# Hybrid attention and experts on one core: token scales carried through DRAM, and third layers that catch up every other step

## The chip, the cores and the metric

The kernel runs on one core of a Trainium2 chip. The metric is the device time of one execution in microseconds. The kernel before takes 3328.4 us (median of three runs, 3327.84 to 3328.48). Its profile shows an execution of 3332.1 us.

The core has five engines that run side by side, each in its own program order: TensorE (PE in the profile, with its weight loads as PEld), VectorE (DVE), ScalarE (ACT), GpSimd (POOL) and SyncE (SP), which here only issues transfers. Data is float32 throughout.

## The reference, cut to what matters

The input is eight images of 256 channels by 32 x 32 pixels. Layer 0 is a pooled attention. Layer 1 turns each image into 1024 tokens of 256 channels, and adds an attention and then a mixture of eight experts:

```
t = tokens(x)                                   # (8, 1024, 256)
t = t + attn(ln_t(t))                           # one head of 256
t = t + ffn(ln_t(t))
ln_t(v): (v - mean) / sqrt(var + 1e-5)          # over the 256 channels of a token
attn(h): softmax(q k^T / 16) v,  q, k, v = h W^T + b
ffn(h):  w = softmax(mean_b(h) Wr + br)         # (1024, 8), one gate per token and expert
         y_e = relu(bn(relu(bn(h W1_e)) W2_e)) Wo_e + bo_e
         sum over e of w_e y_e
```

The change touches the division by the standard deviation in both ln_t, and the order in which the experts' third layer (Wo_e) is worked off.

## The kernel before

A tile of t holds channels in the partitions (two blocks of 128) and tokens along the free dimension. So a token's factor 1/sqrt(var + eps) has to be multiplied into every partition of one column. The mean needs no work here, since it is folded into the weights that follow.

scale_tokens does this. TensorE transposes the tile, VectorE takes statistics of each token (bn_stats), and statistics ends with the power -0.5 on GpSimd. The result r has tokens in the partitions: r[p, t] belongs to token 128 t + p. To turn it into a row that all partitions have, GpSimd builds diag, the identity times r, and TensorE multiplies it by a matrix of ones. Every output row then holds the factors of 128 tokens for each block, in PSUM. VectorE multiplies the tile by it. There are two callers. layer1 scales a whole image of 1024 tokens (two products of 512 columns). norm scales a quarter of 256 tokens after attention (one product of 256 columns, four times an image).

The program is written out by a planner. Work comes in generators (threads) that yield what they need next: an engine, the tiles that have to be ready, and for TensorE a PSUM slot. The class Flow keeps an expected time for every engine and tile (note, cost), and its order becomes the order of the instructions; each engine then works strictly in that order. For a transfer, note adds a lag after its issue until its tile counts as ready.

The attention of layer 0 sets the beat. Its loop has 384 steps: eight images, two channel groups, two halves, twelve blocks of keys. In each step TensorE forms four score products (sc), ScalarE takes their exponential (pt), and TensorE multiplies the block before by the values (pv). After each step f.step lets the threads put in other work up to a credit: convolutions and norms of the next image, and layer 1 of the images that are done (keys "y,t", values "p,v", 32 quarters in all). What is not placed by the end of the loop comes in a tail, where the experts already start so that TensorE is filled. The exponentials' sums are formed on VectorE and, for part of the blocks, by accumulating transfers issued on GpSimd's queue (pt<-pt).

The experts run in units of one expert and 512 tokens, 128 units. first7 and second are the first two layers, in seven half-width products (a Strassen form) of 256 columns each; early ones use a plain form of four products of 512. sums puts the seven products together on VectorE, and combined forms the differences for the next layer, on GpSimd or VectorE. third is the third layer. It needs the gates, which need all images' tokens, so at the end of the tail some 25 units have their first two layers done and wait, stored in DRAM (h2d). The main loop of experts then works off this backlog: weighed fetches, multiplies by the gate (weigh) and combines, and thirds runs one third layer. While the backlog is larger than two (many), every second layer is followed by an extra third layer.

Of the kernel before, what the change touches and what calls it, by code (L numbers as in the profile page):

```python
# [11 lines left out]
ALU = mybir.AluOpType  # L12
# [4 lines left out]
P = 128  # L17
C = 256
HW = 1024
# [636 lines left out]
class Flow:  # L656
# [90 lines left out]
    def note(self, engine, op, ins, args, kwargs):  # L747
        aps = [a for a in (*args, *kwargs.values()) if hasattr(a, "tensor") or hasattr(a, "space")]
        out = kwargs.get("out", args[0] if args else aps[0])
        srcs = [a for a in aps if a is not out]  # L750
        prev = self.last.get(engine)
        if prev is not None:
            self.tc.add_manual_dep(
                ins.ins,
                prev,
                mybir.DependencyInfo(mybir.DependencyClass.NoSync, mybir.DependencyReason.DATA),
                reason="program order",
            )
        self.last[engine] = ins.ins.name
        start = self.now[engine]  # L760
        names = [n for a in srcs for n in self.keys(a)]
        outs = self.keys(out)
        for n in (*names, *outs):
            if self.writer.get(n) != engine:
                start = max(start, self.ready.get(n, 0.0))
        for o in outs:
            if self.reader.get(o, engine) != engine:
                start = max(start, self.read.get(o, 0.0))
        cost = self.cost(engine, op, out, srcs)
        if engine == "PE":  # L770

            tiling = None if op == "transpose" else self.tiling(srcs)
            if tiling != self.tiled:
                cost += {None: 0.09, "rows": 0.2, "columns": 0.13}[tiling]
                self.tiled = tiling

        wide = [a for a in srcs if a.space != PSUM and a.free_size() > 4]
        if "dma" not in op and engine == "POOL" or engine == "DVE" and wide and (len(wide) > 1 or op in ("tensor_scalar", "tensor_copy")):
            start = max(start, self.port)
            self.port = start + cost  # L780
        self.now[engine] = end = start + cost
        lag = 0.15
        if "dma" in op:
            size = 4e-3 * out.shape[0] * out.free_size() if out.space != DRAM else 4e-3 * srcs[0].shape[0] * srcs[0].free_size()
            lag = 2.0 + 0.0045 * size if engine == "SP" else 1.5 + 0.0078 * size
        for n in {*outs, self.key(out)}:
            self.ready[n] = max(self.ready.get(n, 0.0), end + lag)
            self.writer[n] = "DMA" if "dma" in op else engine
        self.open.difference_update(names)
        for n in {*names, *map(self.key, srcs)}:  # L790
            self.read[n] = max(self.read.get(n, 0.0), end + lag)
            self.reader[n] = engine
# [85 lines left out]
        return need[0] is not None and (need[2] is None or self.free(need[2]) < NEVER)  # L878


def attention(tc, kit, f, outer, ended, nb, consts, x, t1, t2, hn, bounds, vecs, q_t, kv_t, proj_t, gqk_t, wqk, wqkv, vecs1, w1_d, w1c, gate_d, wrc, vecs2, bnvec):

# [5 lines left out]
    with ExitStack() as ctx:  # L888
        l1, shared = outer
# [4 lines left out]
        def T(pool, shape, tag, bufs=1):  # L894
            return f.tile(pool, shape, tag, bufs=bufs)
# [60 lines left out]
        def mix():  # L956
# [43 lines left out]
            r = T(wp, [P, 2], "war")  # L1000
# [19 lines left out]
            for c in range(2):  # L1020
                f.pe.transpose(ps[:, c * P : (c + 1) * P], bd[:, c, :], ident)
            yield ve(ps)
            bdt = T(l1, [P, 2, P], "diag4")
            f.ve.tensor_copy(bdt, ps[:, :C].rearrange("p (c q) -> p c q", c=2))
            yield pe(bdt, tag="sm")
            ps = small()
# [36 lines left out]

        def pool(*tiles):
            return "POOL", tiles, None

        def until(cond):
            return None, cond, None
# [168 lines left out]
        def statistics(st, n, eps, mean=None):  # L1237


            var = T(l1, [P, n], f"var{n}")  # L1240
            dev = T(l1, [P, n], f"dev{n}")
            if mean is not None:
                f.ve.tensor_tensor(mean, st[:, :, 1], st[:, :, 4], ALU.add)
            f.ve.tensor_tensor(dev, st[:, :, 1], st[:, :, 4], ALU.subtract)
            f.ve.tensor_tensor(var, st[:, :, 2], st[:, :, 5], ALU.add)
            f.ve.tensor_tensor(dev, dev, dev, ALU.mult)
            f.ve.scalar_tensor_tensor(var, dev, C / 4.0, var, ALU.mult, ALU.add)
            r = T(l1, [P, n], f"rstd{n}", bufs=3)
            rstd(r, var, eps, 1.0 / C)
            return r  # L1250
# [292 lines left out]
                f.sp.dma_start(t1[b], last)  # L1543
            projected[0] += 1

        def scale_tokens(src, n):

            tiles = n // P
            st = T(l1, [P, tiles, 6], f"st{tiles}")
            for g in range(0, tiles, 2):  # L1550
                yield pe(src, tag="sm")
                ps = small()
                for u in range(2):
                    for c in range(2):
                        o = u * C + c * P
                        f.pe.transpose(ps[:, o : o + P], src[:, c, (g + u) * P : (g + u + 1) * P], ident)
                yield ve(ps)
                for u in range(2):
                    f.ve.bn_stats(st[:, g + u, :], ps[:, u * C : (u + 1) * C])
            yield ve(st)  # L1560
            r = statistics(st, tiles, 1e-5)
            for g in range(0, tiles, 4):
                m = min(4, tiles - g)
                yield pool(r)
                diag = T(l1, [P, m, P], f"diag{m}")
                f.pool.tensor_tensor(
                    diag,
                    ident[:, None, :].to_broadcast([P, m, P]),
                    r[:, g : g + m].unsqueeze(2).to_broadcast([P, m, P]),
                    ALU.mult,  # L1570
                )
# [11 lines left out]
        def layer1():  # L1583

            for b in range(nb):
                yield until(lambda: projected[0] > b and ready)
                t = T(l1, [P, 2, HW], "t")
                f.sp.dma_start(t, t1[b])
                yield from scale_tokens(t, HW)
                yield until(lambda: written[0] >= 4 * b)  # L1590
                v = T(l1, [P, 8, C], "v")
                for g in range(4):
# [91 lines left out]

        def norm(b, q, o):

            yield from scale_tokens(o, C)
            f.sp.dma_start(hn[b][:, :, q], o)
            scaled[0] += 1
            written[0] += 1  # L1690
            ended[0] = written[0] // 4
# [123 lines left out]
        for i in range(len(steps) + 1):  # L1815
            if i < len(steps):
                b, c, half, kc = steps[i]
# [171 lines left out]
def experts(tc, kit, nb, t2, hn, h2d, w1c, w2_d, wo_d, bnvec, bo_d, gate_d, wrc, consts8, gtd, out, f, outer, ended, early):  # L1989
# [12 lines left out]
    with ExitStack() as ctx:  # L2002
        l1, shared = outer
# [4 lines left out]
        T = f.tile  # L2008
# [330 lines left out]
        while n3 < total:  # L2339
            many = n2 > n3 + 2  # L2340
            if n2 < n1 - 1 or n1 == total and n2 < total:
                second(n2, many)
                n2 += 1
                if many:
                    weighed(f.pool)
                    thirds()
            weighed(f.ve if many else f.pool)
            if n1 < total:
                first7(n1)
                n1 += 1  # L2350
            thirds()
# [3 lines left out]
def tile_conv_attn_hybrid(  # L2355
# [41 lines left out]
    bnvec = T(cpool, [P, 4 * 2 * NE], "bnvec")  # L2397
    bounds = [T(cpool, [P, NBOUND], f"bound{i}") for i in range(2)]
    flag = T(cpool, [P, 1], "flag")
    last = partial(experts, tc, kit, nb, t2, hn, h2d, w1c, w2_d, wo_d, bnvec, bo_d, gate_d, wrc, consts8, gtd, out)  # L2400
    with ExitStack() as early:
        l1 = early.enter_context(tc.tile_pool(name="l1", bufs=1, side="right"))
        shared = early.enter_context(tc.tile_pool(name="psum_l1", bufs=1, space=PSUM, side="right"))
        f = Flow(tc, kit)

        ended = [0]
        attention(
            tc, kit, f, (l1, shared), ended, nb,
            consts, x, t1, t2, hn, bounds, vecs0, q_t, kv_t, proj_t, gqk_t, wqk, wqkv, vecs1, w1_d, w1c, gate_d, wrc, vecs2, bnvec,
        )  # L2410
        last(f, (l1, shared), ended, early)
# [122 lines left out]
```

## Time and profile before

| stage | from, us | to, us | TensorE busy, us | VectorE busy, us |
| --- | --- | --- | --- | --- |
| start | 0 | 400 | 316.0 | 277.0 |
| attention of layer 0 with layer 1 between | 400 | 1975 | 1510.9 | 1207.2 |
| change to the tail | 1975 | 2050 | 62.7 | 33.7 |
| tail of layer 1 with experts | 2050 | 2280 | 230.0 | 112.9 |
| catch-up of third layers | 2300 | 2575 | 262.1 | 249.4 |
| experts in step | 2625 | 2900 | 274.0 | 216.9 |

In the lines below, the part with numbers 1 to 40 slices the span; a digit is the busy share of a slice in tenths. A line of a stretch gives its length, then for each engine the busy time and in brackets the number of instructions, the granted clock of TensorE, the share of the transfer engines and GB/s. A line of a group gives the engine, the operation, output and inputs by name, the shapes, the count, the busy time, the mean of one in ns and the idle time just before. A line of transfers gives the issuing queue, the count, the size and the time from issue to landing. A TensorE product of float32 is recorded as two pieces, and a piece's recorded length overlaps the next one's. All operations carry the line of the planner's helper, L669, so one goes by the names of tiles.

### The profile page before, as it was taken

The numbers are of one execution on the slowest core, as the hardware profiler recorded it, in microseconds if no ns is written. First come the engines' busy times: TensorE is split into PE (matmuls) and PEld (weight loads), VectorE is DVE, ScalarE is ACT, GpSimd is POOL, SyncE is SP. The second block draws the span as 40 slices with busy tenths as digits, with TensorE's granted clock in tenths as the row PEclk, the third lists the DMA queues.
The fourth block names the chain that finished last, engine by engine and source line by source line (L and its number), as shares of the span: only waits on it lengthen the run. The fifth ranks groups of instructions, "written<-read, shape, count | busy, mean of one in ns | idle before, by whom it ended". The sixth has DMA issues, their size and how long they took to land.

```text
span 3332.1 us, 42942 instructions
## 1 busy us (share of the span) xinstructions
PE 3137.4 (94%) x15970; PEld 1912.8 (57%) x15970; DVE 2472.4 (74%) x4069; ACT 1734.4 (52%) x2328; POOL 1227.3 (37%) x1300
## 2 busy tenths in 40 slices
PE   8687899999999999899899999999999999999997
PEld 4332244344344344344345346777888888888886
DVE  5687788786887886886884555446998787787776
ACT  4476676666576566576566543333233444444442
POOL 2211413213213214213211112006666776777775
PEclk9798999999999999999999999999999999999999
DMA  2357656656646646656556656124442010000000
GB/s 74 82 121 158 131 106 146 133 101 154 133 100 157 135 104 147 135 120 123 121 125 133 133 119 237 70 88 159 158 146 102 20 45 26 20 20 32 20 13 21
DMA packets 106666, 347.10 MB, mean 104 GB/s; under 512 B 13056, under 2 KB 38408, under 8 KB 83216
## 3 DMA queue, kind: packets, MB, share of 16 engines
q0 software_dynamic: 28608, 179.85, 28.1%
q1 hardware_dynamic: 74480, 162.45, 14.1%
q8 instruction: 128, 2.10, 0.3%
q10 hardware_dynamic: 3360, 1.97, 0.2%
q14 instruction: 90, 0.74, 0.1%
HBM read 105.11 MB, written 73.97 MB: 54 GB/s over the span
## 4 chain that ended last, share of the span: by engine, by line
PE 57%; DVE 5%; issue 3%; ACT 3%; POOL 3%; DMA 2%; SPq 0%; DVEq 0%; POOLq 0%; ACTq 0%
PE bank L669 18%; PE sm L669 13%; PE y L669 8%; PE sc L669 6%; PE sx L669 6%; PE pv L669 5%; DVE h L669 2%; ACT pt L669 2%; POOL tm L669 1%; DVE u L669 1%; DMA pt<-pt 1%; ACT h L669 1%; POOL t L669 1%; DVE t L669 1%; DVE c L669 1%
## 5 line engine op out<-in xcount | busy, mean ns | idle before, releaser
L669 ACT ACTIVATE pt<-sc 128x2048 f32<-128x2048 f32 (+1 forms) x384 | 719.9, 1875 | 326.5 <-PE sc L669 272.7
L669 DVE SCALAR_TENSOR_TENSOR acc<-p,vec,acc 128x225 f32<-128x225 f32 (+7 forms) x928 | 526.6, 574 | 29.3 <-ACT acc L669 4.8
L669 PE MATMUL sc<-q,kn 32*128 32x512 f32 (+1 forms) x3072 | 445.6, 650 | 94.7 <-ACT pt L669 92.9
L669 DVE TENSOR_TENSOR pt<-pt,pt 128x1024 f32<-128x1024 f32 x320 | 387.4, 1254 | 144.3 <-DMA pt<-pt 135.3
L669 POOL DMA_DIRECT2D pt<-pt x192 | 174.0, 907 | 780.1 <-ACT pt L669 615.7
L669 PE MATMUL pv<-pt,vt 128*32 128x512 f32 (+1 forms) x3072 | 420.6, 620 | 0.0
L669 ACT ACTIVATE p1c<-bank 128x256 f32<-128x256 f32 x228 | 87.2, 383 | 576.4 <-PE bank L669 576.1
L669 ACT ACTIVATE h<-h,bnvec 128x512 f32<-128x512 f32 x456 | 345.0, 805 | 50.7 <-DVE h L669 43.7
L669 POOL TENSOR_TENSOR rstd<-rstd,mhalf 128x4 f32<-128x4 f32 (+2 forms) x88 | 107.0, 1216 | 673.8 <-DVE rstd L669 635.0
L669 DVE TENSOR_TENSOR h<-p1c,bank 128x512 f32<-128x512 f32 x228 | 155.2, 681 | 194.7 <-PE bank L669 191.2
L669 PEld LDWEIGHTS sc<-q,kn 32*128 32x128 f32 (+1 forms) x3072 | 116.1, 178 | 285.8 <-ACT pt L669 184.9
L669 POOL TENSOR_TENSOR tm<-h,tm 128x256 f32<-128x256 f32 x206 | 247.6, 1202 | 16.1
L669 DVE TENSOR_TENSOR h<-u,bank 128x256 f32<-128x256 f32 x456 | 232.1, 550 | 7.9
L669 PEld LDWEIGHTS pv<-pt,vt 128*32 128x32 f32 (+1 forms) x3072 | 60.7, 108 | 301.7 <-issue 290.3
L669 POOL TENSOR_TENSOR tm<-h 128x512 f32<-128x512 f32 x103 | 133.9, 1300 | 245.2 <-ACT h L669 241.2
L669 DVE TENSOR_TENSOR h<-h,gate 128x1024 f32<-128x1024 f32 x128 | 209.1, 1642 | 2.5 <-DMA h<-h 2.1
L669 PE MATMUL bank<-h,w2e 128*128 128x256 f32 (+1 forms) x612 | 198.8, 453 | 4.1 <-DVE h L669 4.1
L669 PE MATMUL y<-t,s3e 128*128 128x256 f32 x768 | 188.0, 381 | 10.6 <-POOL t L669 10.3
L669 POOL TENSOR_TENSOR t<-h,t 128x256 f32<-128x256 f32 x210 | 177.4, 845 | 16.5
L669 PE MATMUL bank<-t,s1e 128*128 128x256 f32 x750 | 182.3, 379 | 0.0
L669 PE MATMUL sm<-y,t 128*128 128x256 f32 x752 | 180.6, 385 | 0.0
L669 DVE TENSOR_TENSOR u<-h,bank 128x512 f32<-128x512 f32 x228 | 156.7, 687 | 24.0
(316 smaller groups left out, 5604.3 us busy)
## 6 DMA issues: line engine op xcount, KB each, us to landing
pt<-pt POOLq DMA_DIRECT2D x160, 1024.0 KB, 7.4
h<-h SPq DMA_DIRECT2D x90, 512.0 KB, 3.2
xi<-in_x_dram SPq DMA_DIRECT2D x16, 512.0 KB, 6.7
t<-t SPq DMA_DIRECT2D x8, 1024.0 KB, 9.7
res<-t SPq DMA_DIRECT2D x32, 256.0 KB, 3.9
t<-res SPq DMA_DIRECT2D x32, 256.0 KB, 5.4
hn<-res SPq DMA_DIRECT2D x32, 256.0 KB, 3.0
hn<-hn SPq DMA_DIRECT2D x16, 512.0 KB, 4.2
```

Source lines behind the costliest of these rows:

```text
L669: ins = fn(*args, **kwargs)
```

## The change

It has two parts. For the first six images, scale_tokens no longer forms diagonals. SyncE stores r into a row in DRAM in token order, and loads it back broadcast to all 128 partitions (256 or 512 tokens at a time, into one buffer named rb); VectorE multiplies by that. TensorE and GpSimd have no part in it. The last two images keep the diagonal products, which answer sooner. The planner is told to count 8 us for each of these transfers. The diag tiles of the remaining cases move into the same buffer rb.

In the experts, the extra third layer comes only with every other second layer while a backlog is there, and VectorE and GpSimd change places in who combines for it.

```
 def scale_tokens(src, n, b):
     ...
     r = statistics(st, tiles, 1e-5)
+    if b < nb - 2:
+        row = kit.tile(dram, [1, n], f"dev_row{kit.n}")
+        yield sp(r)
+        f.sp.dma_start(row.rearrange("o (t p) -> (o p) t", p=P), r)
+        yield sp(row)
+        w = min(512, n)
+        for o in range(0, n, w):
+            rb = T(l1, [P, w], "rb")
+            f.sp.dma_start(rb, row[:, o : o + w].to_broadcast([P, w]))
+            yield ve(rb)
+            d = src[:, :, o : o + w]
+            f.ve.tensor_tensor(d, d, rb[:, None, :].to_broadcast([P, 2, w]), ALU.mult)
+        return
     for g in range(0, tiles, 4):
         m = min(4, tiles - g)
         yield pool(r)
-        diag = T(l1, [P, m, P], f"diag{m}")
+        diag = T(l1, [P, m, P], "rb")
         ...
 # Flow.note
             lag = 2.0 + 0.0045 * size if engine == "SP" else 1.5 + 0.0078 * size
+            if "dev_row" in (self.key(out) + "".join(map(self.key, srcs))):
+                lag = 8.0
 ...
 # main loop of experts
                 second(n2, many)
                 n2 += 1
-                if many:
-                    weighed(f.pool)
+                if many and n2 % 2:
+                    weighed(f.ve)
                     thirds()
-            weighed(f.ve if many else f.pool)
+            weighed(f.pool)
```

More of the change, by code (lines that the diff above doesn't have):

```diff
@@ L878, in possible, with attention @@
         return need[0] is not None and (need[2] is None or self.free(need[2]) < NEVER)
-def attention(tc, kit, f, outer, ended, nb, consts, x, t1, t2, hn, bounds, vecs, q_t, kv_t, proj_t, gqk_t, wqk, wqkv, vecs1, w1_d, w1c, gate_d, wrc, vecs2, bnvec):
+def attention(tc, kit, f, outer, ended, nb, dram, consts, x, t1, t2, hn, bounds, vecs, q_t, kv_t, proj_t, gqk_t, wqk, wqkv, vecs1, w1_d, w1c, gate_d, wrc, vecs2, bnvec):
     nc = tc.nc
@@ L1022, in mix @@
             yield ve(ps)
-            bdt = T(l1, [P, 2, P], "diag4")
+            bdt = T(l1, [P, 2, P], "rb")
             f.ve.tensor_copy(bdt, ps[:, :C].rearrange("p (c q) -> p c q", c=2))
@@ L1065, in pool, with sp @@
             return "POOL", tiles, None
+        def sp(*tiles):
+            return "SP", tiles, None
         def until(cond):
@@ L1544, in project, with scale_tokens @@
             projected[0] += 1
-        def scale_tokens(src, n):
+        def scale_tokens(src, n, b):
             tiles = n // P
@@ L1588, in layer1 @@
                 f.sp.dma_start(t, t1[b])
-                yield from scale_tokens(t, HW)
+                yield from scale_tokens(t, HW, b)
                 yield until(lambda: written[0] >= 4 * b)
@@ L1685, in norm @@
         def norm(b, q, o):
-            yield from scale_tokens(o, C)
+            yield from scale_tokens(o, C, b)
             f.sp.dma_start(hn[b][:, :, q], o)
@@ L2407, in tile_conv_attn_hybrid @@
         attention(
-            tc, kit, f, (l1, shared), ended, nb,
+            tc, kit, f, (l1, shared), ended, nb, dram,
             consts, x, t1, t2, hn, bounds, vecs0, q_t, kv_t, proj_t, gqk_t, wqk, wqkv, vecs1, w1_d, w1c, gate_d, wrc, vecs2, bnvec,
```

## The prediction

> **What bounds the kernel now.** I read the page's first two parts, then busy time in chosen stretches, then groups by shape, then TensorE's timeline.
>
> ```profile
> PE 3137.4 (94%) x15970; PEld 1912.8 (57%) x15970; DVE 2472.4 (74%) x4069; ACT 1734.4 (52%) x2328; POOL 1227.3 (37%) x1300
> PE   8687899999999999899899999999999999999997
> DVE  5687788786887886886884555446998787787776
> ```
>
> TensorE is the bound, but a soft one before 1975 us (attention, slices 1 to 24). The stretches show where:
>
> ```profile
> core 0: us, PE busy (x) PEld busy (x) DVE busy (x) ACT busy (x) POOL busy (x), PEclk, DMA share, GB/s
> 1425.00:1600.00 175.00, 174.16 (x953) 86.72 (x950) 137.44 (x254) 115.73 (x150) 48.88 (x57) 1.00 0.60 129
> 1600.00:1650.00 50.00, 40.77 (x261) 13.58 (x259) 44.58 (x75) 28.74 (x27) 12.12 (x14) 1.00 0.62 130
> ...
> 2050.00:2280.00 230.00, 230.00 (x903) 164.96 (x903) 112.94 (x209) 90.42 (x154) 19.04 (x29) 0.99 0.29 102
> 2300.00:2350.00 50.00, 44.38 (x202) 37.66 (x201) 41.69 (x52) 13.13 (x22) 44.36 (x53) 1.00 0.38 129
> 2350.00:2575.00 225.00, 217.71 (x996) 187.81 (x995) 207.74 (x263) 69.35 (x115) 139.57 (x119) 1.00 0.39 138
> ```
>
> Inside an image TensorE has no gap (174.16 of 175). Where one image passes to the next it idles 9.2 of 50 us while VectorE works 44.6. After attention, in the tail of layer 1 filled with experts, it is never idle (230.00 of 230). In the catch-up of the third layers (2300 to 2575) it idles 5.6 + 7.3 = 12.9 us; VectorE is at 91%, and in the first 50 us GpSimd at 89%.
>
> What a product costs is read from starts, not from the busy column:
>
> ```profile
> 2012.91 3.60 PE L669 MATMUL bank<-h,w2e 128*128 128x512 f32 x8
> 2016.34 3.60 PE L669 MATMUL bank<-hn,w1e 128*128 128x512 f32 x8
> ```
>
> Eight pieces of 512 columns start 3.43 us before the next eight; a product is two pieces, so 0.86 us, and 0.43 us for 256 columns.
>
> **What the Trainium skill says.** "SBUF — State Buffer", Who interferes with whom: a VectorE instruction with two SBUF inputs contends with a GpSimd instruction that reads SBUF. The trace agrees: the weighing h<-h,gate takes 1.64 us in the mean and 1.29 us at 2327.95. "DMA: Bandwidth & Descriptors", Rules for kernel authors: a strided last dimension becomes one descriptor per element, and a transfer that reads what another wrote must wait for that one's semaphore. The row is written with a stride, so I count 128 x 8 = 1,024 descriptors for a whole image, 256 for a quarter, and two trips in series. No run so far shows such a store.
>
> **The change part by part.**
>
> *Diagonals out.* Six images lose two products of 512 columns and four of 256: 6 x (2 x 0.86 + 4 x 0.43) = 20.6 us of TensorE. GpSimd loses their building:
>
> ```profile
> L669 POOL TENSOR_TENSOR diag<-con,rstd 128x256 f32<-128x256 f32 x32 | 26.4, 825 | 1.1
> L669 POOL TENSOR_TENSOR diag<-con,rstd 128x512 f32<-128x512 f32 x16 | 19.5, 1220 | 33.3 <-PE sm L669 28.5 <-PE sx L669 4.7
> ```
>
> 12 x 1.22 + 24 x 0.83 = 34.5 us, but GpSimd is 37% busy. It matters only where a diag stands ahead of an accumulating pt transfer: at 1617.11 and 1629.52 it delays one by 1.0 to 1.3 us, the second on the chain. I take 0.5 us an image, -3 us (0 to -12).
>
> The two wide products of an image mostly fall into the stretch where TensorE idles anyway (the fourth image's at 1155.96 and 1161.65, in a slice of 25 us with 21.4 busy), so their 10.3 us are half worth nothing; the narrow ones lie where it is full.
>
> *Transfers in.* Each use now pays a store of the row and a broadcast load. Nearest rows:
>
> ```profile
> pt<-pt POOLq DMA_DIRECT2D x160, 1024.0 KB, 7.4
> ...
> hn<-res SPq DMA_DIRECT2D x32, 256.0 KB, 3.0
> ...
> gate<-gtd SPq DMA_DIRECT2D x16, 256.0 KB, 5.1
> ```
>
> The load has the size and form of gate<-gtd: 5.1 us. The store is at least hn<-res's 3.0; for an upper end, hardware queue packets take 14.1% x 16 x 3332 / 74480 = 0.10 us each, and 1,024 over 16 engines are 64, or 6.5 us. So 8 to 12 us together against the 8 + 8 that the planner now allows. VectorE, which multiplies in program order with the convolution and the pt sums queued behind it, should find the row landed: I cost that wait at nothing. The store can hold up the pt transfers, for whose landing VectorE already idles 135.3 us in all; 0 to 6 x 6.5 us if every one hit the chain, and I take +1. On the SP queue the row's wait stands ahead of res, t, q and xi loads; the planner issues these up to 10 us ahead, so nothing.
>
> The multiply itself reads the row from SBUF, not PSUM: 12 of t at 1.215 us and 24 of res at 0.68 become two-input ones; if GpSimd blocks half by 0.4 us, 7 us of VectorE, mostly beside other work.
>
> *What moves.* The order in which the changed program's instructions stand shows more than the diff. Ahead of the last score product, TensorE has 12 products of 512 and 25 of 256 from diagonals less (21.1 us), but also 60 products of 256 columns of layer 1 less, with their small companions (28.8 us). Layer 1 waits longer for each row, so two of its 32 quarter units slip from attention into the tail. The loop loses 49.9 us, the tail gains 29.2 for them, and two second layers more run in plain form (4 x 0.86 against 7 x 0.43, 0.84 us). The whole program: -20 us.
>
> The tail is full, so its +30 us count in full. What the loop gives back I estimate so: an attention step runs from one group of score products to the next, 384 in all. I price TensorE's work of each step from starts as above (1.0 us for a group of four tiled products) and set it against the step's time in the trace. Steps with over 3.4 us of work last 1.05 times the tally; the 57 with under 2.6 us (from the 61st step on) still last 3.36 us, because ScalarE's exponential (1.88) and the score group that it waits for (1.07) and follows are a floor. In the changed order the steps under 2.2 us rise from 66 to 96. Mapping each step's work to time gives -21.5 us; a floor of 3.14 to 3.37 us gives -28 to -23. A third tally, by quarters of an image, takes VectorE's work between the same pt sums as another floor: two quarters now carry 58 and 60 us of it, above TensorE's 53 and 57, and the loop gains only some 14 to 18. I take **-25**, the middle of the step tallies: half the work that leaves the loop leaves a hole.
>
> *Catch-up every other step.* Before, a catch-up step has four layers of TensorE (4 x 3.02 = 12.1 us) and on VectorE two sums of 2.47, two weighings of 1.65, one combination (1.06 + 2 x 0.84), and a share 2/8 of a tile's end (4.95) plus 0.2: 12.4 us. VectorE is over the bound, as 91% busy with bursts says. After, two steps hold seven layers, 21.1 us, and 9.9 + 5.0 + 2.7 + 1.9 + 0.4 = 19.9 us. Most of the 7.3 us idle after 2350 should go. The 5.6 before 2350 stay: GpSimd builds s3e and s2e there (2.5 and 2.0 us each) beside tm and t (4.0 + 3.5), per two steps 26.5 us against 21.1. **-7** (-2 to -11). 26 more second layers go through DRAM (52 more h transfers); with the DMA share at 0.39 they hide.
>
> Sum: -25 (loop) + 30 (tail) - 7 (catch-up) - 3 (GpSimd) + 1 (transfers) = -4, so 3328.4 becomes **3324**.
>
> **The rivals.**
>
> *Faster* (0.27). The loop hands over most of the work taken out: holes are filled since rows land in 10 us, not 16, and the quarters even out. Loop -38, tail +30, catch-up -10: 3310. For it: inside images TensorE has no gap, 174 of 175. Against: the program's order is fixed beforehand; a row landing early moves no product forward.
>
> *Slower* (0.28). VectorE's crowded quarters set the pace: loop -14, tail +30, catch-up -4, transfers +3: 3343. For it: VectorE already works 44.6 of 50 us at the passages, and the rows are brought just there. Against: the count of 8 + 8 us is generous.
>
> *Near balance* (0.45): 3324, give or take 8.
>
> **How the numbers follow.** Faster by over 0.2% means under 3321.7, slower over 3335.1. The balance case puts 0.19 under, 0.23 between, 0.03 above; rivals add 0.27 below, 0.03 between and 0.25 above. So 0.46, 0.26, 0.28. The range 3306 to 3344 leaves out the fast rival's far end and the slow one's.
>
> **What would show it.** Right: the last score product earlier by 20 to 28 us (from 1968), the first y product about 6 later (from 2280); TensorE's idle between 400 us and the last score product up from 64 to about 90; idle in the catch-up at 6 of some 500 us; stores landing in 3 to 7 us and no VectorE wait of over 2 us on rb. Wrong: the loop shorter by over 35 us (holes filled), by under 15 (VectorE's floor), or VectorE waiting on rb, which would make the allowance of 8 us too small.

## The result, and the profile after

The changed kernel takes 3413.8 us (median of four runs, 3406.0 to 3416.2), the kernel before 3328.4: a ratio of 1.0249, 95% interval 1.0229 to 1.0269. It is 85 us slower. I had forecast 3324, 4 us faster, with 3344 as the upper end of the range.

The page of the changed kernel, the same lines as were shown of before: engine totals, and the slices of TensorE and VectorE.

```profile
PE 3149.0 (92%) x15886; PEld 1908.9 (56%) x15886; DVE 2441.4 (72%) x4064; ACT 1735.1 (51%) x2326; POOL 1160.7 (34%) x1255
PE   8687799899999989989989988999999999999997
DVE  5687686786887886786874534545788888777776
```

There are 84 fewer records of TensorE products (two to a product), and yet TensorE is busy 12 us longer, in a span that is 78 us longer. Between slices 6 and 23 TensorE's row had two 8s, now it has four. The time has gone into the attention, with TensorE both idle and slower.

Two marks cut each profile into three stages: the last score product (sc<-q,kn) ends the attention's loop, the first product of a third layer (y<-h,wo) ends the tail. TensorE's idle time is the stretch's length less its busy time.

| stage | before, us | after, us | difference | forecast |
| --- | --- | --- | --- | --- |
| loop: 0 to the last score product | 1968.2 | 2028.2 | +60.1 | -25 |
| tail: to the first y product | 311.9 | 353.3 | +41.4 | about +30 |
| rest: to the end of the span | 1052.0 | 1028.6 | -23.4 | about -7 |
| TensorE idle from 400 us to the last score product | 64.1 | 140.6 | +76.5 | +26 |

These are the stretches themselves, first the loop of before from 400 us on and its tail, then loop and tail of after (columns as ahead of the prediction):

```profile
400.00:1968.16 1568.16, 1504.06 (x8550) 694.75 (x8548) 1204.37 (x2102) 1005.43 (x1211) 369.00 (x432) 0.99 0.59 127
1968.16:2280.00 311.84, 299.51 (x1153) 206.97 (x1153) 149.40 (x263) 111.92 (x189) 36.44 (x66) 0.98 0.39 133
```

```profile
400.00:2028.21 1628.21, 1487.66 (x8324) 667.03 (x8321) 1178.22 (x2078) 997.14 (x1188) 335.58 (x394) 0.96 0.63 126
2028.21:2381.40 353.19, 341.85 (x1331) 240.47 (x1331) 167.00 (x291) 127.02 (x217) 35.11 (x61) 0.98 0.36 125
```

The tail carries 42 us more of TensorE work (341.85 against 299.51 before) and is 41 us longer, so it is as full as before. In the loop TensorE has 226 records of products fewer. By the prediction's count they are worth 49.9 us, but the busy time falls by 16.4 only: the rest of the work ran some 33 us slower, at a granted clock of 0.96 in place of 0.99. So -50 of work, +76 of idle time and +33 of slower running give the +60. (The 33 is what remains in this sum, not a measurement of its own.)

The transfers that the change brought, from the profile's full list of issues (queue, count, size of one, median us to landing), and the waits on them over the whole run (engine and what it waited for: us in all, times, longest):

```profile
rb<-dev_row SPq DMA_DIRECT2D x12, 256.0 KB, 5.4
rb<-dev_row SPq DMA_DIRECT2D x24, 128.0 KB, 6.4
...
dev_row<-rstd SPq DMA_DIRECT2D x24, 1.0 KB, 8.2
...
dev_row<-rstd SPq DMA_DIRECT2D x6, 4.0 KB, 10.9
```

```profile
DVE res L669 <- DMA rb<-dev_row: 6.7, 2, 5.6
...
DVE t L669 <- DMA rb<-dev_row: 2.0, 1, 2.0
```

```profile
SPq L669 <- DMA dev_row<-rstd: 236.5, 28, 17.9
SPq L669 <- POOL rstd L669: 221.7, 26, 26.8
```

A store of 1 KB takes longer to land than a load of 256 KB. VectorE hardly waits for rb, 8.7 us in all. The SP queue stands 236 us for rows to land and 222 us for their source. At the same time other waits of this queue fell: those for ScalarE's pool and VectorE's res were 718 and 643 us before, and are 479 and 475. And these waits grew, before first, then after:

```profile
DVE pt L669 <- DMA pt<-pt: 135.3, 62, 8.3
...
PE sc L669 <- ACT pt L669: 92.9, 92, 3.6
...
ACT pt L669 <- DMA pt<-pt: 17.5, 9, 3.2
```

```profile
DVE pt L669 <- DMA pt<-pt: 176.0, 74, 8.5
PE sc L669 <- ACT pt L669: 151.4, 115, 7.3
...
ACT pt L669 <- DMA pt<-pt: 51.5, 14, 6.8
```

pt<-pt is the attention's accumulating transfer. ScalarE and VectorE wait for its landing, and TensorE's next score product waits for ScalarE. From this view came three theories:

- Theory 1: the stores, in pieces of 4 bytes, hold up the accumulating transfers.
- Theory 2: the SP queue stands waiting for rows or their source, and the loads of q, xi, t and res stand behind it.
- Theory 3: the planner's order, which the lags of 8 us changed, costs in itself, whatever the transfers do.

### The profile page after: what moved, and what is told of

It is laid out like the page before. It is cut to its first block, busy times and chain, and to the rows that moved or that the text cites. A ratio compares the mean times of both kernels' runs of the same rounds, so it can differ in the third digit from the quotient of the medians.

```text
span 3410.1 us, 42908 instructions
## 1 busy us (share of the span) xinstructions
PE 3149.0 (92%) x15886; PEld 1908.9 (56%) x15886; DVE 2441.4 (72%) x4064; ACT 1735.1 (51%) x2326; POOL 1160.7 (34%) x1255
## 5 line engine op out<-in xcount | busy, mean ns | idle before, releaser
L669 PE MATMUL sc<-q,kn 32*128 32x512 f32 (+1 forms) x3072 | 461.2, 671 | 156.0 <-ACT pt L669 151.4
L669 DVE SCALAR_TENSOR_TENSOR acc<-p,vec,acc 128x225 f32<-128x225 f32 (+7 forms) x928 | 518.5, 565 | 29.6 <-ACT acc L669 4.7
L669 PE MATMUL pv<-pt,vt 128*32 128x512 f32 (+1 forms) x3072 | 430.8, 634 | 0.0
L669 POOL TENSOR_TENSOR tm<-h,tm 128x256 f32<-128x256 f32 x202 | 235.7, 1167 | 15.9
L669 DVE TENSOR_TENSOR h<-h,gate 128x1024 f32<-128x1024 f32 x128 | 201.3, 1573 | 0.5 <-ACT h L669 0.5
L669 PE MATMUL sm<-p,v 128*128 128x256 f32 x800 | 188.6, 388 | 0.0
L669 PEld LDWEIGHTS sm<-p,v 128*128 128x128 f32 x800 | 152.6, 194 | 46.7 <-issue 25.7
```

The source lines that it names most:

```text
L669: ins = fn(*args, **kwargs)
```

## The experiments

"Before" was run again beside each group of kernels (medians 3328.0 to 3334.9), so the ratios are what to compare; 1% is 33 us. A cost in us is from the ratio or from the medians, which differ by up to 2 us. The stage marks are from one profiled execution of each, and that can lie 8 us off its median (before: 3334.6 against 3328.4; e17: 3349.8 against 3356.3).

| kernel | loop, us | tail, us | rest, us | ratio, interval |
| --- | --- | --- | --- | --- |
| before | 1968.2 | 311.9 | 1052.0 | |
| after | 2028.2 | 353.3 | 1028.6 | 1.0249 (1.0229 to 1.0269) |
| e1 rows alone | 2039.3 | 354.3 | 1043.5 | 1.0326 (1.0304 to 1.0348) |
| e2 contiguous store | 1981.8 | 353.3 | 1028.8 | 1.0116 (1.0098 to 1.0133) |
| e3 load waits for no row | 2063.0 | 353.9 | 1028.7 | 1.0332 (1.0314 to 1.0349) |
| e4 both | 1984.0 | 356.4 | 1028.5 | 1.0107 (1.0090 to 1.0124) |
| e5 catch-up alone | 1966.1 | 314.8 | 1044.2 | 0.9973 (0.9959 to 0.9987) |
| e6 diagonals, lag of 16 us | 1978.4 | 335.5 | 1047.9 | 1.0097 (1.0076 to 1.0117) |
| e7 contiguous, default lag | 2034.2 | 310.3 | 1044.6 | 1.0159 (1.0138 to 1.0179) |
| e8 row by transpose | 2024.6 | 313.5 | 1044.5 | 1.0166 (1.0145 to 1.0187) |
| e9 before + stores of 4 bytes | 2043.2 | 308.1 | 1051.9 | 1.0235 (1.0211 to 1.0259) |
| e10 before + contiguous stores | 1965.7 | 310.5 | 1051.2 | 1.0012 (1.0003 to 1.0022) |
| e11 no wait on SP | 1971.9 | 353.5 | 1028.1 | 1.0104 (1.0080 to 1.0129) |
| e12 diagonals, lag of 4 us | 1948.5 | 326.6 | 1058.2 | 1.0028 (1.0020 to 1.0035) |
| e13 six stores of 4-byte pieces | 2002.8 | 309.5 | 1052.0 | 1.0111 (1.0094 to 1.0128) |
| e14 twenty-four such stores | 2015.8 | 308.5 | 1051.5 | 1.0168 (1.0148 to 1.0188) |
| e15 thirty stores of 128 pieces | 2016.4 | 313.2 | 1051.1 | 1.0167 (1.0148 to 1.0187) |
| e16 4-byte pieces 64 bytes apart | 1961.0 | 308.7 | 1051.3 | 1.0003 (0.9993 to 1.0014) |
| e17 loads of 32 bytes | 1966.2 | 353.1 | 1028.7 | 1.0074 (1.0054 to 1.0094) |
| e18 lag of 16 us and catch-up | 1981.2 | 335.5 | 1039.3 | 1.0086 (1.0067 to 1.0105) |

### The store, the wait, or both taken away from the changed kernel

**e1**, the change without its edit to the experts' loop:

> The row transfers and the planner's lag of 8 us, with the third layers catching up at every step as before. If the two halves of the change add, and the catch-up is worth the -11 us that the stretch after the first y product lost beyond the moved work (-23.4 + 12.1), this half alone gives 3414 + 11 = 3425 us. The rival, that the catch-up's new engines are part of the harm (its adds on VectorE delaying what the attention left over), gives 3400 us or less.

Measured 3441.2 us, 1.0326: the rows alone do all the harm, and the catch-up's edit is no part of it. The sum of 3425 was missed by 16. TensorE's order up to the first y product is that of the changed kernel, but this loop was 11 us longer. By the ratios e1 is 26 us behind the changed kernel, give or take 10, and the rest explains 15 of them; the other 11 stay unexplained.

**e2**, the row stored as a partition holds it:

```
-f.sp.dma_start(row.rearrange("o (t p) -> (o p) t", p=P), r)
+f.sp.dma_start(row.rearrange("o (p t) -> (o p) t", p=P), r)
```

> The changed kernel with the row stored in the order in which a partition holds it: 128 pieces of 32 or 8 bytes in place of 1,024 or 256 of 4 bytes; same instructions in the same order (the factors reach other tokens than their own). Theory 1, the pieces of 4 bytes hold up the accumulating transfers of the attention: the 57.9 us that VectorE's, ScalarE's and TensorE's waits grew in the attention mostly go, landing falls from 8.2 to 3 to 4 us, time 3340 to 3355 us. Theory 2, the SP queue stands behind the row (236 us of waiting for it, 222 us for its source): only the first shrinks, by half, and about a quarter of the 85 us comes back: 3390 us. Theory 3, the planner's changed order costs whatever the transfers do: 3405 to 3414 us.

Measured 3368.9 us, 1.0116. The other way of writing the same 1 or 4 KB gives back 1.33% (1.0249 - 1.0116), 44 us, all of it in the loop (2028.2 to 1981.8; tail and rest stay). The landing, from the same list of its profile:

```profile
dev_row<-rstd SPq DMA_DIRECT2D x24, 1.0 KB, 3.7
...
dev_row<-rstd SPq DMA_DIRECT2D x6, 4.0 KB, 1.4
```

Theory 1 is at work, but 39 us over before remain, more than it alone allows. (The factors reach other tokens than their own here; the instructions and their order are the changed kernel's.)

**e3**, the loads made independent of the stored row, and **e4**, e2 and e3 together:

```
-f.sp.dma_start(rb, row[:, o : o + w].to_broadcast([P, w]))
+...                                              # two lines that keep the planner's order
+f.sp.dma_start(rb, w1_d[0:1, 0].rearrange("o u c -> o (u c)")[:, :w].to_broadcast([P, w]))
```

> The changed kernel in which the broadcast loads read a fixed row of a weight, so that no load waits for a stored row to land; the rows are still stored piece by piece, all in the same order (the factors are thus those of the weight). Theory 1 (the pieces of 4 bytes): nothing comes back, 3405 to 3414 us. Theory 2 (the SP queue): its 236 us of waiting for rows go, the 222 us for the source stay; about half of the 85 us comes back: 3370 us. Theory 3 (the planner's order): 3405 to 3414 us.

> The changed kernel with both of the edits before: rows stored in 128 pieces, loads from a fixed row. Theory 1: as with the store alone, 3340 to 3355 us. Theory 2: as with the load alone or a little better, 3365 us. Theory 3, the planner's order in itself: still 3400 us or more.

Measured 3443.3 us (1.0332) and 3368.6 us (1.0107). e4 is e2 again, within the intervals, though the 101 us for which e2's SP queue still stood for rows are gone. So that standing cost nothing that can be measured. e3 takes away all 236 us and gives nothing back, but it cannot price them, for it brings something new. It is even longer than the changed kernel, by 35 us in the loop. Its loads, now issued right behind the slow store, land late, in 11.9 us at the median (128 KB) where e4's land in 4.2 behind the quick one. Waiting for the row had kept the loads out of the store's way; that this is where the 35 us went was not tried.

### Each half of the rest by itself

**e5**, the other half of the change alone, put into the kernel before:

```
-                if many:
-                    weighed(f.pool)
+                if many and n2 % 2:
+                    weighed(f.ve)
                     thirds()
-            weighed(f.ve if many else f.pool)
+            weighed(f.pool)
```

> The kernel before with the catch-up's edit alone: third layers at every other step of the many, added on VectorE, the closing ones on GpSimd; diagonals as before. In the changed kernel the stretch after the first y product is 14.9 us shorter than in the one with the rows alone (1043.5 to 1028.6), while the whole time differs by 27 us. If only the stretch counts and the halves add: 3313 to 3318 us, 0.3 to 0.45% faster than before. Rival, that all of the 27 us belong to it: 3301 us. Rival, that it helped only where the rows had shifted work: 3328 us.

Measured 3324.1 us against 3331.4, 0.9973 (0.9959 to 0.9987): 7 us by the medians, 9 by the ratio, and 7.8 are seen in the rest (1052.0 to 1044.2). That is a little less than the 0.3 to 0.45% expected. This is the quickest kernel of the study, ahead of both the kernel before and the changed one.

**e6**, the kernel before with its diagonals, and its planner told that the deviations are 16 us late (**e12**: 4 us):

```
 r = statistics(st, tiles, 1e-5)
+f.ready[r.name] += 16.0 * (n == HW or written[0] < 4 * (nb - 2))
```

> The kernel before, diagonal products and no transfers, in which the planner is told that each deviation is ready 16 us later than it is, as the lags of 8 us for store and load tell it in the changed kernel. Theory 3 (the planner's order: layer 1's units come later, slip into the tail, and crowd what is left): what is left with contiguous stores, 36 us over before less the catch-up's -15, so 3360 to 3380 us. Rival, that the remainder is the broadcast loads' traffic and the stores that are left: 3328 to 3340 us.

> The kernel before, with diagonals, each deviation reckoned 4 us late in place of the 16 us that cost 33 us. If the cost goes with the delay: a quarter, 3335 to 3340 us. If any reshuffle of a planned order costs, whatever its size: 3350 to 3365 us. If a little delay fits better: under 3328 us.

Measured 1.0097, 32 us, for 16 us of lag, and 1.0028, 9 us, for 4. No transfer is added here and no product taken out; only the order differs. (The edit delays the whole-image deviations of all eight images, where the change touches six.) In e6 the tail is 24 us longer: counted by products, some 18 us of layer 1 have slipped into it and 6 of expert work have moved up. The loop should be shorter by those 18 us and is 10 us longer. Theory 3 holds: an order that counts on late rows costs 32 us by itself, where e2, which has the catch-up's gain in it, has 39 left. A quarter of the lag cost about a quarter, but not in the same place: in e12 the same 18 us have slipped, and its loop does end 20 us earlier.

**e7**, e2 with the two lines of the planner's lag taken out again:

```
-            if "dev_row" in (self.key(out) + "".join(map(self.key, srcs))):
-                lag = 8.0
```

> The changed kernel with the contiguous store and without the planner's special lag of 8 us: it now reckons 2.0 us for the store and 2.6 to 3.2 us for the load, where the contiguous rows landed in 3.7 us and the loads in 5.1 to 6.9 us. Theory 3 (the order): layer 1 is planned about 11 us earlier per unit, less slips into the tail, 3335 to 3350 us. Rival, that the lag is needed: VectorE and TensorE stand where the rows come later than planned, 3369 us or more.

Measured 3386.4 us, 1.0159, worse than e2. The units no longer slip (tail 310.3), but now VectorE stands in its program order for rows that are not there:

```profile
DVE res L669 <- DMA rb<-dev_row: 90.7, 16, 12.4
...
DVE t L669 <- DMA rb<-dev_row: 28.7, 6, 8.9
```

119 us in 22 waits, where the changed kernel had 8.7 in three. So the lag was needed. Too long costs order, too short costs waits.

**e8**, each row turned round on TensorE and stored in whole pieces:

```
+...                                              # yields and tiles left out, here and below
+f.pe.transpose(ps[:tiles, :P], r, ident)
+f.ve.tensor_copy(rt[:tiles], ps[:tiles, :P])
-f.sp.dma_start(row.rearrange("o (t p) -> (o p) t", p=P), r)
+f.sp.dma_start(row.rearrange("o (t p) -> (o t) p", p=P), rt[:tiles])
```

> The changed kernel in which TensorE turns the deviations round first (one transpose and one small copy on VectorE for each row), so that each row is stored in 8 or 2 pieces of 512 bytes, each factor at its own token. Theory 1 (pieces of 4 bytes hold up the attention's transfers): about as with the contiguous store, 3365 to 3375 us; if even 128 pieces of 8 or 32 bytes still held something up, down to 3355 us. If only the number of stores and loads counted: 3414 us.

Measured 3384.8 us, 1.0166, 10 us over the expected window. Loop and tail together are e2's (2024.6 + 313.5 = 2338.1 against 2335.1). What differs is the rest, 1044.5 against 1028.8: here no expert work slipped ahead of it. It is a way to keep the rows at their own tokens and still store them cheaply, but not one that beats the diagonals.

### The stores put into the kernel before

The next runs leave every engine's order as in the kernel before (TensorE, VectorE, ScalarE and GpSimd instruction by instruction), and only add stores on the SP queue:

```
 r = statistics(st, tiles, 1e-5)
+if b < nb - 2:
+    row = kit.tile(dram, [1, n], ...)
+    ...
+    f.sp.eng.dma_start(row.rearrange("o (t p) -> (o p) t", p=P), r)     # e9;  e10: "o (p t) -> (o p) t"
```

> The kernel before, its diagonals and the order of every engine untouched, with the 30 rows stored as well, in pieces of 4 bytes, to rows that nobody reads. Theory 1: it loses by itself what the contiguous store gave back, 45 us: 3365 to 3380 us. Rival, that the pieces hurt only in the changed order or through the loads that wait for them: 3328 to 3340 us.

> The same with the rows stored in 128 pieces of 8 or 32 bytes: the kernel before, all engines in its order, plus 30 stores for whose source the SP queue waits as in the changed kernel. Theory 1: 3328 to 3335 us. Rival, theory 2 in its other half (the SP queue stands 222 us for the deviations, with the loads of q, xi, t and res behind): 3340 to 3355 us, and the run before it holds that too.

e9: 3406.3 us, 1.0235. Thirty stores of 4-byte pieces, 48 KB in all, which nobody reads, cost 77 us, and the time lies 26 us over the window expected. e10: 3334.6 us, 1.0012, 4 us, though the SP queue stands 159 us for the same sources (e9: 168 us). So it is not the standing queue, theory 2's other half, and it is not the number of stores.

One store shows how. In e9 the first image's store is issued at 403.57 us, two pt<-pt transfers at 403.5 and 406.2. The pt tile between 403 and 417 us, e9 (line, engine, operation, count: shortest/median/longest ns, first and last start) and its landing; then the two that the kernel before issues in the same stretch:

```profile
L669 POOL DMA_DIRECT2D pt<-pt x2: 882/895/908, 403.5 to 406.2; - x2
...
DMA to landing us min/median/max: 13.9/15.0/16.1
```

```profile
L669 POOL DMA_DIRECT2D pt<-pt x2: 880/894/908, 409.8 to 413.9; - x2
...
DMA to landing us min/median/max: 7.2/7.8/8.3
```

They land after 13.9 and 16.1 us in place of 7.2 and 8.3. The stretches from this store on, in e9:

```profile
403.50:413.50 10.00, 8.95 (x52) 2.45 (x48) 9.36 (x22) 4.70 (x5) 3.91 (x5) 1.00 1.14 69
413.50:418.50 5.00, 0.10 (x1) 0.00 (x0) 3.50 (x4) 1.64 (x4) 0.00 (x0) 0.93 0.89 185
418.50:423.50 5.00, 3.96 (x16) 0.72 (x16) 2.43 (x3) 1.98 (x2) 0.87 (x1) 0.50 0.94 193
```

For 10 us the transfer engines count as fully busy (1.14; a packet counts in full where it starts, so this can pass 1) and move 69 GB/s; only then do the accumulations come through, at 185. By that time TensorE stands: 0.10 of 5 us. And when it goes on, its clock is 0.50. In the timeline the score group after the stall takes 2.09 us, the one ahead of it 1.14:

```profile
410.40 1.14 PE L669 MATMUL sc<-q,kn 32*128 32x512 f32 x8
...
419.42 2.09 PE L669 MATMUL sc<-q,kn 32*128 32x512 f32 x8 [5.82 <-ACT pt L669]
```

A half clock after a stall isn't the store's doing as such. The kernel before has one nearby, without any store, after an idle time of 3.63 us:

```profile
403.30 1.14 PE L669 MATMUL sc<-q,kn 32*128 32x512 f32 x8
...
409.07 2.09 PE L669 MATMUL sc<-q,kn 32*128 32x512 f32 x8 [3.63 <-ACT pt L669]
```

Idle times of 2.34 us, in e10 and e16 at the place of e9's long stall, are followed by groups of 1.14 us.

Over all 28 places where e9's loop issues a store (two places hold two), I took the longest landing of a pt<-pt issued from 3 us before to 7 us after: its median is 13.2 us in e9, 8.8 in e10. Two places of the Trainium skill bear on this. "DMA: Bandwidth & Descriptors", Issuing engines are not separate DMA queues: transfers of all issuing engines run on the same 16. The trace agrees: a store from SP's queue delays GpSimd's. "TensorE: Matmul & The Clock Gate", Part 1: after an idle window of about 3.4 us the clock falls to half until it has been busy for as long. The trace agrees here: half clock after 5.82 and 3.63 us, none after 2.34. The slow running then lasted some 9 and 6 us, longer than the page's window. So a long stall costs more than its own length. e9 has the work of the kernel before, and its loop is 75.0 us longer; 51.9 of that is idle time (116.0 against 64.1; 33.1 of it longer waits for ScalarE's pt, 56.2 to 89.3) and 23.1 is more busy time for the same products (1527.17 against 1504.06):

```profile
400.00:2043.17 1643.17, 1527.17 (x8535) 700.64 (x8531) 1200.88 (x2099) 1002.76 (x1206) 369.95 (x432) 0.97 0.65 122
```

**e13 to e16** ask what it is in such a store. They add to the kernel before the six whole-image stores alone, the 24 quarter stores alone, all 30 with only their first column (128 pieces of 4 bytes), and all 30 with the pieces 64 bytes apart:

```
+    f.sp.eng.dma_start(row.rearrange("o (t p) -> (o p) t", p=P)[:, 0:1], r[:, 0:1])         # e15
+    f.sp.eng.dma_start(row.rearrange("o (t p s) -> (o p) t s", p=P, s=16)[:, :, 0], r)      # e16, a row of 16 n
```

> The kernel before in its own order plus only the six stores of whole images in pieces of 4 bytes, 6 x 1,024 = 6,144 pieces. If each piece costs the same: half of 77 us, 3367 us. If each store costs the same: 6 of 30, 15 us, 3344 us.

> The kernel before in its own order plus only the 24 stores of quarter images in pieces of 4 bytes, 24 x 256 = 6,144 pieces, as many as the six stores have. If each piece costs the same: 3367 us. If each store costs the same: 24 of 30, 61 us, 3390 us.

> The kernel before in its own order plus 30 stores of 128 pieces of 4 bytes (the first column of the deviations alone). If the number of pieces counts: 3,840 pieces, no more than the contiguous store has, 3330 to 3336 us. If pieces of 4 bytes, or that each partition's piece lies right beside its neighbour's, is what holds the engines: 3350 us or more.

> The kernel before in its own order plus the 30 stores with all their pieces of 4 bytes, each 64 bytes from the next in place of side by side. If the number of pieces is what counts: 3406 us as with them side by side. If it is that neighbouring pieces fall into one stretch of memory: 3330 to 3350 us.

e13: 3366.4 us, 1.0111, 37 us. e14: 3383.1, 1.0168, 56 us. The same 6,144 pieces, and neither reckoning fits: a whole-image store costs 6.2 us (37 / 6), a quarter's with a quarter of the pieces 2.3 (56 / 24). Together the two cost more than all thirty do, 93 us against 77. e15: 3383.2, 1.0167, 56 us with only 128 pieces a store, which e10's stores have too, at 4 us. So the number of pieces is not the cause. With 128 pieces in each store, the landing at the median falls as the pieces grow: 8.7 us with 4 bytes (e15), 4.0 with 8 and 1.4 with 32 (e10). e16: 3330.5 us, 1.0003 (0.9993 to 1.0014): with all the pieces of 4 bytes, 1,024 or 256 a store, the cost is gone as soon as they lie 64 bytes apart. The landing of the stores, in e15 and then e16:

```profile
dev_row<-rstd SPq DMA_DIRECT2D x30, 0.5 KB, 8.7
```

```profile
dev_row<-rstd SPq DMA_DIRECT2D x24, 1.0 KB, 1.7
...
dev_row<-rstd SPq DMA_DIRECT2D x6, 4.0 KB, 2.8
```

And the stretch from its first store on (at 407.24 us, pt<-pt at 407.2 and 409.8), e16:

```profile
407.20:417.20 10.00, 8.95 (x52) 2.45 (x48) 9.39 (x22) 4.74 (x5) 3.88 (x5) 1.00 0.94 181
417.20:422.20 5.00, 2.20 (x17) 0.47 (x16) 4.96 (x6) 3.69 (x4) 0.87 (x1) 1.00 0.55 111
```

The same 52 instructions of TensorE in the same 8.95 us, but 181 GB/s go through beside the store in place of 69, and the clock stays at 1.00. The packets of these two stretches, by queue (packets, MB, share of 16 engines; q0 is GpSimd's queue, q1 SP's), in e9 and then in e16:

```profile
q0 software_dynamic: 84, 0.69, 108.9%
q1 hardware_dynamic: 1040, 0.00, 4.6%
```

```profile
q0 software_dynamic: 236, 1.80, 89.4%
q1 hardware_dynamic: 1040, 0.00, 4.6%
```

The store's own packets take 4.6% of the engines' time in the slow form and in the quick one. What changes is the other queue: a packet of pt<-pt takes 2.07 us in the mean (1.089 x 160 / 84) in place of 0.61. What holds the accumulating transfers up is 4-byte pieces that lie side by side, and it can't be read from the time of the pieces' packets.

### What is left without the stores

**e11**, e4 with the store's source a constant too, so that SP waits neither for a row nor for its source; **e17**, e11 with each load cut to 32 bytes for each partition, which the multiply reads over and over; both in the changed kernel's order. **e18**, e6 and e5 together:

```
-f.sp.dma_start(row.rearrange("o (p t) -> (o p) t", p=P), r)
+f.sp.dma_start(row.rearrange("o (p t) -> (o p) t", p=P), ident[:, :tiles])              # e11
 ...
+f.sp.dma_start(rb[:, :8], w1_d[0:1, 0].rearrange("o u c -> o (u c)")[:, :8].to_broadcast([P, 8]))   # e17
```

> The changed kernel with contiguous stores of a constant and loads of a fixed row, so that the SP queue waits neither for the deviations nor for a landing; all engines in the order of the changed kernel (the factors are those of a weight). Theory 2 in its other half: the 238 us of waiting for the source go, 3345 to 3355 us. If the planner's order is all that is left: 3369 us again.

> The run without waits on SP, and each broadcast load cut to 8 numbers (32 bytes) for each partition in place of 256 or 512, read again and again by the multiply (the factors are those of a weight); all engines in the order of the changed kernel. If the 6.0 MB of the loads hold something up: 3335 to 3350 us. If the planner's order is what is left: 3355 to 3365 us.

> The kernel before with diagonals, each deviation reckoned 16 us late, and the catch-up at every other step: no row transfers. If order and catch-up add: 1.0097 + 0.9973 - 1, so 3351 us. If the removal of the diagonal products were worth its 20.6 us on TensorE, this would lie that much above the run before it.

e11: 3362.9 us, 1.0104, between the two times expected; e17: 3356.3, 1.0074; e18: 3360.1, 1.0086, where e5 and e6 add up to 1.0070, within noise of it. From e2 to e11 to e17 the ratio falls by 0.1% and 0.3%. The intervals of e2 and e17 do not overlap, so the SP queue's standing and the loads' 6 MB are together worth some 14 us, give or take 9; one by one they are not told from noise. e17 has cheap stores, tiny loads, no wait, no diagonal products for six images and the catch-up's edit; e18 has all its diagonal products, no transfers and the same edit. They agree within their intervals. So in a delayed order the removal of 20.6 us of TensorE work bought nothing that can be measured (4 us by the ratios, give or take 9). The two orders aren't the same one, and e17 still has its thirty stores and small loads, so this is an agreement, not a proof.

## Why the prediction was wrong, point by point

- **"The store can hold up the pt transfers ... 0 to 6 x 6.5 us ... and I take +1": this is the step that failed.** The mechanism was named; the term was mis-sized. In the order of before the stores cost 77 us (e9), in the changed order 44 (after against e2); why less there was not tried. Three errors made it small. The landing was reckoned from mean packets of 0.10 us, 3.0 to 6.5 us in all; it was 8.2 and 10.9. In the stretch shown the store's own packets take 0.007 us each (0.046 x 160 / 1040), so no count of packets leads to its cost. The reckoning took a piece to cost the same wherever it lies; e15 and e16 show that it does not, and the packets by queue that the cost falls on another transfer. I let only the six large stores count; the 24 small ones, with as many pieces together, cost more (56 us against 37). And out of 0 to 39 us I took +1 without giving a reason.
- **"Half the work that leaves the loop leaves a hole": -25 for the loop: failed as well, by 23 us.** With stores, loads and waits out of the way (e17) the loop ends at 1966.2 us, 2 us earlier than before, though 49.9 us of work left it. Nearly all of it left a hole. The price of a late order is in e6. My tally let a step last as long as steps of about the same work did before. Done again on the traces of three other orders, with the same prices and from the 61st step on, it says -21 us for e17, where +1 was measured, and -6 for e6, where it was +16: in both, steps of equal work last 22 us longer in all. For e12, with its lag of 4 us, it says -14, and -14 was measured. (In the order of before itself, e10 and e16 are up to 5 us off.) So the floor for short steps was right, and what failed is that it and the 1.05 were taken over unchanged into an order laid for late rows. TensorE's wait for ScalarE's pt in the loop, 56.2 us before, is 76.5 in e6 and 91.3 in e17; what makes ScalarE late there wasn't tried. The rival that named VectorE's crowded quarters (loop -14, 3343 us) had the side right and the size far off, and whether VectorE is the cause stays open.
- **Together** the loop's +60 reads: -2 (e17, where -25 was forecast), +6 to e11 for the loads' full size, +10 to e2 for the waits on SP, +46 from e2 to after for the pieces side by side. The middle two are single profiles, within what such loops vary.
- **The tail, +30, and that it counts in full: right.** It carries 42 us more and is 41 longer. The 12 us beyond 30 are expert work that moved ahead of the first y product (12.9 us by its products), which the prediction's count of the tail left out, and they are missing from the rest.
- **The catch-up, -7 (-2 to -11): right.** Alone 9 us (4 to 14 by the interval, e5). In the changed kernel, TensorE idles 1.2 + 2.2 us in the two stretches that lost 12.9 before, where I had left 5.6. The backlog now lasts longer; from 2400 to 2900 us it idles 5.5, and the sign named was 6 of some 500:

```profile
2400.00:2450.00 50.00, 48.83 (x222) 41.34 (x221) 45.41 (x59) 17.05 (x28) 46.74 (x59) 1.00 0.42 147
2450.00:2675.00 225.00, 222.83 (x1031) 195.51 (x1031) 187.75 (x263) 78.22 (x130) 138.59 (x135) 1.00 0.41 146
```

- **VectorE's wait on rb costed at nothing: nearly right**, 8.7 us in three waits, the longest 5.6 where I had said none over 2. e7 shows that the allowance of 8 + 8 us was what kept it so.
- **"On the SP queue the row's wait stands ahead of res, t, q and xi loads ... so nothing": right in cost.** The queue stood 458 us in all, while its waits for pool and res fell by 407. e4 and e10 put the price of that at a few us.
- **GpSimd's relief, -3: not tried by itself**, and e17 beside e18 could not show a term of that size.
- **VectorE's multiplies, +7 if GpSimd blocks half: too much.** The 24 of res rose from 0.683 to 0.757 us in the mean, the 12 of t from 1.215 to 1.220: 1.8 us. The example for it, the weighing of 1.29 us at 2327.95, was badly chosen, for GpSimd works beside it nearly all the time. Over the 128 weighings the trace does agree: 1.22 us in the 14 with no GpSimd instruction beside them, 1.69 in the others.
- **The range, 3306 to 3344, was too narrow** because the store's term was bounded by a formula, and its upper end, 39 us, was then left out of the range although the trace held no such store at all.

## What to carry to other kernels

Before data is stored through an access pattern, look where its pieces land: 4-byte pieces from different partitions side by side in DRAM took some 10 us a store here, and what paid was another queue's transfer that the engines were waiting for. The same bytes laid out so that each partition writes 8 bytes or more, or each piece 64 bytes from the next, were nearly free. An operation that a planner is told to expect late can cost time through the order, even when it costs nothing itself: imitate the delay alone, without the change, before building the change. And of two edits that come together, run each alone; here the small one was the gain.

## What the runs showed of the hardware that was not expected

- Stores of 256 or 1,024 four-byte pieces side by side land in 8.2 us at the least (median 10.1, e9; the trace has the landing of 20 of the 30); with 64 bytes from piece to piece the same stores land in 1.7 and 2.8 us at the median. The Trainium skill says in "DMA: Bandwidth & Descriptors", Specifications, that transfers under 512 bytes become read-modify-write. Both forms are far below that, and only one is slow, so size alone doesn't decide here. That neighbouring pieces wait for each other's read-modify-write would fit, but no run shows it; distances between 4 and 64 bytes were not tried. Pieces of 8 bytes side by side were quick (e10: 4.0 us at the median).
- In the 10 us behind one such store the engines count as busy and move 69 GB/s, where 181 go through beside the spread one. Its own packets take 4.6% of the engines' time either way; the other queue's take three times as long each, 2.07 us against 0.61.
- Idle times of TensorE of 5.82 us (e9) and 3.63 us (before) were followed by score groups of 2.09 us in place of 1.14; after 2.34 us (e10, e16) they were not. In e9, 23 of 75 us lost are slower products, not waiting.
